# Cutting the later loads of a DMA-bound kernel into pieces of 16 rows and dealing them out between the stores

## The chip, the cores and the metric

One core of a Trainium2 chip runs the kernel. The metric is the device time of one execution in microseconds (us). All runs quoted here are of the fast state; profiles are one execution each, and a span in a profile is some 2 us shorter than the time of the same execution. "The queue" below is SyncE's instruction stream, which issues nearly all transfers (SPq in the profile); "the engines" without a name are the 16 DMA engines.

## The reference, cut to what matters

```python
_pairs = list(itertools.combinations(range(32), 2))        # 496 pairs (i, j)
v_i = inputs[:, I_IDX, :]                                   # inputs (1024, 32, 128)
v_j = inputs[:, J_IDX, :]
transformed = jnp.einsum('bpd,ped->bpe', v_i, W)            # W (496, 128, 128)
return transformed * v_j                                    # (1024, 496, 128), 260 MB
```

## The kernel before

Each pair is computed in two halves (steps u = 0 to 991) of 512 batch rows: TensorE multiplies, VectorE multiplies by the second field and writes an output tile, and after the second half SyncE stores that tile of 512 KB. All x stays on the chip once loaded; W comes in 62 chunks of eight pairs (512 KB) through three buffers. The parts that the change touches:

```python
opool = ctx.enter_context(tc.tile_pool(name="o", bufs=6))

def load_x(f, n=1, pieces=1, eng=None): ...       # t[:, :, ...] <- xt[:, f:f+n, ...], 1 MB for n=2
def load_w(c, splits=(0, WL)): ...                # w_raw[c] <- wt[c], 512 KB

# ... start-up loads ...
load_w(1)
load_x(NF - 6, 2)
# ... split_w, split_x, first(u) cut ...
def second(u):
    # ...
    nc.vector.tensor_tensor(ots[g][:, k, s], po.pop(u), x_sb[j][:, s], ALU.mult)
    # ...
    elif k == OG - 1 and h == 1:
        nc.sync.dma_start(out=out[g], in_=ots[g])

for u in range(2 * NQ + LAG):
    q = u // 2
    if u % (2 * WL) == 0 and (q // WL + WLEAD) * WL < NQ:
        load_w(q // WL + WLEAD)                   # every 16 steps
    if u < 2 * NQ:
        i, j = pairs[q]
        if u % 2 == 0 and j == i + 1 and i % 2 == 0 and 0 <= i - 2 - XLEAD:
            load_x(i - 2 - XLEAD, 2)
        first(u)
    if u >= LAG:
        second(u - LAG)
    # ...
```

## Time and profile before

| | before |
|---|---|
| median of the runs beside the changed kernel | 781.52 us (778.96 to 786.6) |
| profiled span | 775.5 us |
| bytes read, written | 49.3 MB, 260.0 MB |
| transfers issued by SyncE | 577 |
| DMA packets of the main queue, share of 16 engines | 83,088, 100.4% |

The DMA shares of the slices and stages say whether the engines are the bound; they are shown in the prediction. The timeline of the queue alone over 12 us (start, length, engine, line, operation, tile, count; a length over several instructions includes the gaps between them):

```profile
301.22 1.58 SPq L167 DMA_DIRECT2D out_dram<-ot  x2
302.90 1.09 SPq L83 DMA_DIRECT2D w<-in_wt_dram  x1
304.09 8.16 SPq L167 DMA_DIRECT2D out_dram<-ot  x6
```

The reader sees that the queue carries eight stores and a load in each period. A store's issue after a pause lasts 333 ns in the median of 296 cases, and 1.06 us in the median of 131 when it follows another store without one. From 30 us after the start to 30 us before the last issue, 709 us, issues and the short gaps between them fill 413 us; the other 296 us the queue waits for something to issue. 332 of 494 stores are issued within 0.1 us of the end of the VectorE instruction that completes their tile: mostly the queue waits for VectorE.

### The profile page before, as it was taken

What the parts mean: (1) busy time and instruction counts of PE and PEld (TensorE: products, weight loads), DVE (VectorE), ACT (ScalarE), POOL (GpSimd) and SP (SyncE); (2) the same over time, 40 slices, a digit from 0 to 9 for tenths busy, and PEclk for the clock granted to TensorE, in tenths of its full rate; (3) what the DMA queues carried; (4) which work ended last, traced back from release to release, by engine and by line L of the source; (5) the groups of instructions that cost most, each with busy time, mean ns of one, the idle gap of its engine ahead of it and who ended that gap; (6) DMA issues with size and microseconds to landing.
All of it is one profiled execution on the core that took longest, in us unless ns stands there. A gap on an engine that the chain in (4) does not pass through costs nothing.

```text
span 775.5 us, 11576 instructions
## 1 busy us (share of the span) xinstructions
PE 713.5 (92%) x2946; PEld 559.3 (72%) x2946; DVE 628.8 (81%) x992; ACT 616.6 (80%) x1136; POOL 550.7 (71%) x523
## 2 busy tenths in 40 slices
PE   7899889898997998998998999899999999999994
PEld 3477668786886876776876877688778778777773
DVE  4578769696887977887886897798988988889886
ACT  1279768797896997886986988699889889888883
POOL 0989997978686886875867595668676758585550
PEclk9999989999999999999999999899999999999998
DMA  9999999999999999999999999999999999999997
GB/s 354 418 374 408 416 382 391 403 409 403 403 407 396 408 405 417 393 392 410 409 399 408 393 405 397 394 395 404 411 406 406 409 405 404 414 405 398 410 415 318
DMA packets 83730, 310.10 MB, mean 400 GB/s; under 512 B 9296, under 2 KB 9424, under 8 KB 81872
## 3 DMA queue, kind: packets, MB, share of 16 engines
q1 hardware_dynamic: 83088, 308.32, 100.4%
q10 hardware_dynamic: 576, 1.05, 0.4%
q8 instruction: 23, 0.38, 0.2%
q14 instruction: 43, 0.35, 0.1%
HBM read 49.28 MB, written 260.05 MB: 399 GB/s over the span
## 4 chain that ended last, share of the span: by engine, by line
PE 44%; DMA 38%; DVE 12%; POOL 3%; issue 1%; DVEq 0%; ACT 0%; SPq 0%; POOLq 0%
DMA out_dram<-ot 35%; PE po L148 30%; PE po L157 14%; DVE ot L163 12%; DMA x<-in_xt_dram 2%; POOL xd L109 1%; POOL xl L107 1%; DMA w<-in_wt_dram 1%; POOL wl L93 0%; POOL xl L108 0%; POOL wd L95 0%; DVEq L163 0%; ACT xh L106 0%; POOL wd L94 0%; SPq L83 0%
## 5 line engine op out<-in xcount | busy, mean ns | idle before, releaser
L163 DVE TENSOR_TENSOR ot<-po,x 128x512 f32<-128x512 f32 x992 | 628.8, 686 | 139.5 <-DMA out_dram<-ot 90.7
L149 ACT ACTIVATE po<-po 128x512 f32<-128x512 f32 x962 | 538.9, 581 | 131.7 <-PE po L148 85.4
L148 PE MATMUL po<-xh,wh 128*128 128x512 f32 x962 | 387.0, 402 | 44.5 <-DVE ot L163 44.0
L148 PE MATMUL po<-xl,wl 128*128 128x512 f32 x962 | 380.7, 396 | 3.4 <-POOL wl L93 2.5
L157 PE MATMUL po<-xd,wd 128*128 128x512 f32 x962 | 379.9, 395 | 0.0
L93 POOL TENSOR_TENSOR wl<-w,wh 128x512 fp32r<-128x512 f32 x121 | 156.3, 1292 | 152.5 <-ACT wh L92 152.4
L148 PEld LDWEIGHTS po<-xh,wh 128*128 128x128 f32 x962 | 184.1, 191 | 105.5 <-DVE ot L163 66.3
L148 PEld LDWEIGHTS po<-xl,wl 128*128 128x128 f32 x962 | 184.6, 192 | 40.5 <-POOL wl L93 2.9
L157 PEld LDWEIGHTS po<-xd,wd 128*128 128x128 f32 x962 | 183.6, 191 | 39.8 <-ACT po L149 0.4
L95 POOL TENSOR_TENSOR wd<-wl,wd 128x512 fp32r<-128x512 f32 x121 | 156.7, 1295 | 10.1
L107 POOL TENSOR_TENSOR xl<-x,xh 128x512 fp32r<-128x512 f32 x52 | 67.3, 1293 | 22.8 <-ACT xh L106 22.8
L94 POOL TENSOR_SCALAR wd<-wh 128x512 fp32r<-128x512 f32 x121 | 75.2, 621 | 10.2
L92 ACT ACTIVATE wh<-w 128x512 fp32r<-128x512 f32 x121 | 75.7, 626 | 0.0
L109 POOL TENSOR_TENSOR xd<-xh,xl 128x512 fp32r<-128x512 f32 x52 | 67.0, 1289 | 4.3
L106 ACT ACTIVATE xh<-x 128x512 fp32r<-128x512 f32 x52 | 32.6, 630 | 14.1 <-DMA x<-in_xt_dram 14.1
L108 POOL TENSOR_SCALAR xl<-xl 128x512 fp32r<-128x512 f32 x52 | 32.3, 622 | 4.5
L145 PE MATMUL po<-x,w 128*128 128x512 f32 x60 | 28.7, 642 | 4.2 <-DMA x<-in_xt_dram 4.2
L145 PEld LDWEIGHTS po<-x,w 128*128 128x128 f32 x60 | 11.9, 204 | 20.1 <-issue 13.4
L106 ACT ACT_TABLE_LOAD x1 | 1.3, 1283 | 2.6 <-issue 2.6
L200 POOL MEMSET const-float32-0.0<- 128x1 f32 x1 | 0.1, 99 | 0.2 <-issue 0.2
L200 POOL MEMSET const-bfloat16-1.0<- 128x1 bf16 x1 | 0.1, 102 | 0.0
L200 POOL MEMSET const-uint8-127<- 128x1 uint8 x1 | 0.1, 102 | 0.0
(1 smaller groups left out, 0.1 us busy)
## 6 DMA issues: line engine op xcount, KB each, us to landing
out_dram<-ot SPq DMA_DIRECT2D x494, 512.0 KB, 7.3
w<-in_wt_dram SPq DMA_DIRECT2D x61, 512.0 KB, 7.1
x<-in_xt_dram SPq DMA_DIRECT2D x14, 1024.0 KB, 10.1
x<-in_xt_dram ACTq DMA_DIRECT2D x4, 256.0 KB, 5.7
x<-in_xt_dram SPq DMA_DIRECT2D x2, 512.0 KB, 6.9
out_dram<-ot SPq DMA_DIRECT2D x4, 256.0 KB, 6.1
w<-in_wt_dram SPq DMA_DIRECT2D x1, 448.0 KB, 4.7
w<-in_wt_dram SPq DMA_DIRECT2D x1, 64.0 KB, 3.1
```

The source lines that it names most:

```text
L92: nc.scalar.mul(h, raw, 1.0 - 2.0**-13)
L93: nc.gpsimd.tensor_tensor(l, raw, h.bitcast(F32), ALU.subtract)
L94: nc.gpsimd.tensor_scalar(d, h.bitcast(F32), EPS, 1.0, ALU.mult, ALU.mult)
L95: nc.gpsimd.tensor_tensor(d, l.bitcast(F32), d.bitcast(F32), ALU.subtract)
L106: nc.scalar.mul(h, x_sb[f][:, s], 1.0 - 2.0**-13)
L107: nc.gpsimd.tensor_tensor(l, x_sb[f][:, s], h.bitcast(F32), ALU.subtract)
L109: nc.gpsimd.tensor_tensor(d, h.bitcast(F32), l.bitcast(F32), ALU.subtract)
L145: nc.tensor.matmul(po[u], w_raw[q // WL][:, q % WL, :], x_sb[i][:, s], start=True, stop=True)
L148: nc.tensor.matmul(po[u], w_s[c][t][:, r], x_s[i][t][:, s], start=t == 0, stop=t == 1)
L149: nc.scalar.mul(po[u], po[u], 1.0 + EPS)
L157: nc.tensor.matmul(po[u], w_s[q // WC][2][:, r], x_s[i][2][:, s], start=False, stop=True, skip_group_check=True)
L163: nc.vector.tensor_tensor(ots[g][:, k, s], po.pop(u), x_sb[j][:, s], ALU.mult)
```

## The change

Its intent: a whole load of w leaves 128 data packets and 16 landings in the trace, so, counted evenly, eight packets in a row on each engine: 8 x 159 = 1,272 ns of its time between two stores. A piece of 16 rows leaves 16 data packets and again 16 landings, a single row on each engine, and one piece per step is issued between the stores. A pair takes two steps, so two pieces follow each store while a load is being dealt out.

```diff
     load_w(1)
     load_x(NF - 6, 2)
+    load_w(2)
+    load_x(NF - 8, 2)
+    pieces = []
+    LS = P // 16
+
+    def trickle(dst, src):
+        for k in range(LS):
+            pieces.append((dst[k::LS], src[k::LS]))
+
+    def load_x_slow(f, n):
+        t = xpool.tile([P, n, BT], F32, tag=f"x{f}", name=f"x_{f}")
+        for k in range(n):
+            x_sb[f + k] = t[:, k, :]
+        trickle(t, xt[:, f : f + n, :])
+
+    def load_w_slow(c):
+        w_raw[c] = rpool.tile([P, WL, P], F32, tag="w", name=f"w_{c}")
+        trickle(w_raw[c], wt[c])
@@ the loop over u
-        if u % (2 * WL) == 0 and (q // WL + WLEAD) * WL < NQ:
-            load_w(q // WL + WLEAD)
+        if u % (2 * WL) == 0 and q > 0 and (q // WL + WLEAD) * WL < NQ:
+            load_w_slow(q // WL + WLEAD)
...
-            if ... and i % 2 == 0 and 0 <= i - 2 - XLEAD:
-                load_x(i - 2 - XLEAD, 2)
+            if ... and i % 2 == 0 and i < NF - 2 and 0 <= i - 2 - XLEAD:
+                load_x_slow(i - 2 - XLEAD, 2)
             first(u)
         if u >= LAG:
             second(u - LAG)
+        if pieces:
+            dst, src = pieces.pop(0)
+            nc.sync.dma_start(out=dst, in_=src)
```

More of the change, by code (lines that the diff above doesn't have):

```diff
@@ L170 @@
         q = u // 2
-        if u % (2 * WL) == 0 and (q // WL + WLEAD) * WL < NQ:
-            load_w(q // WL + WLEAD)
+        if u % (2 * WL) == 0 and q > 0 and (q // WL + WLEAD) * WL < NQ:
+            load_w_slow(q // WL + WLEAD)
         if u < 2 * NQ:
             i, j = pairs[q]
-            if u % 2 == 0 and j == i + 1 and i % 2 == 0 and 0 <= i - 2 - XLEAD:
-                load_x(i - 2 - XLEAD, 2)
+            if u % 2 == 0 and j == i + 1 and i % 2 == 0 and i < NF - 2 and 0 <= i - 2 - XLEAD:
+                load_x_slow(i - 2 - XLEAD, 2)
             first(u)
```

## The prediction

> **What bounds the kernel now.** I read the page from the busy shares down, because the change moves only transfers: first who is busiest, then the DMA rows of the slices, then what the engines wait for, and last the single packets.
>
> ```profile
> PE 713.5 (92%) x2946; PEld 559.3 (72%) x2946; DVE 628.8 (81%) x992; ACT 616.6 (80%) x1136; POOL 550.7 (71%) x523
> ...
> DMA  9999999999999999999999999999999999999997
> ...
> DMA packets 83730, 310.10 MB, mean 400 GB/s; under 512 B 9296, under 2 KB 9424, under 8 KB 81872
> ...
> q1 hardware_dynamic: 83088, 308.32, 100.4%
> ...
> HBM read 49.28 MB, written 260.05 MB: 399 GB/s over the span
> ```
>
> No compute engine is full, but the DMA row is at 9 in every slice but the last, and the packets of the one queue that matters take 100.4% of 16 engines' span. The table by stage says the same with decimals (the columns are PE, PEld, DVE, ACT and POOL busy, then clock, DMA share and GB/s):
>
> ```profile
> 0.00:20.00 20.00, 15.85 (x31) 6.58 (x32) 8.53 (x14) 3.30 (x5) 1.48 (x5) 1.00 0.92 356
> 200.00:300.00 100.00, 93.63 (x401) 75.66 (x399) 82.68 (x131) 84.99 (x160) 77.82 (x74) 0.98 1.02 406
> 700.00:775.00 75.00, 63.93 (x274) 50.78 (x273) 62.09 (x98) 55.83 (x101) 31.98 (x30) 0.97 0.97 387
> ```
>
> From 60 to 700 us the share is 1.02: packets overlap a little and no engine has a gap. Only the start and the end fall short. The waits of VectorE and of the queue that issues transfers show how this reaches the engines:
>
> ```profile
> DVE ot L163 <- DMA out_dram<-ot: 90.7, 54, 5.0
> ...
> SPq L167 <- DVE ot L163: 444.2, 458, 5.9
> SPq L167 <- DMA x<-in_xt_dram: 13.9, 8, 2.8
> ...
> out_dram<-ot SPq DMA_DIRECT2D x494, 512.0 KB, 7.3
> w<-in_wt_dram SPq DMA_DIRECT2D x61, 512.0 KB, 7.1
> x<-in_xt_dram SPq DMA_DIRECT2D x14, 1024.0 KB, 10.1
> ```
>
> VectorE waits 90.7 us for an output buffer to be stored; there are six, a store takes 7.3 us to land, and TensorE stands behind VectorE. So the kernel is **bound by DMA engine time**, and I priced that from single packets. Of the 4 KB packets (71,296) the median is 159 ns; of the 8 KB packets (1,792, only x loads) 309 ns; a 4-byte semaphore packet (9,232) takes 9 ns. All packets at such normal durations are 752.3 us of 16 engines. They really took 778.4 us: **26.1 us is excess** in single slow packets, 18.6 us among the 4 KB and 7.3 us among the 8 KB ones, some of them 1 to 2 us long. About 86% of it lies in the stretches from 2.5 us before a load's first landing to its last. In 1 us bins that no load touches the engines move 416 GB/s, in bins full of them 384. That is the gap this change can hope to close: 310.1 MB at 416 GB/s is 745 us, with about 8 us of start and drain 753, or 22 us under the span.
>
> [...]9,296 landings are 16 for each of 581 transfers.
> - [...]This trace's slow packets reach 2.19 us.
> [...]
>
> **The change part by part.**
> 1. *Start: nothing.* The weights' chunk 2 and the x pair for NF-8 were issued at step 0, and still are, in the same order.
> 2. *Added transfers.* Chunks 3 to 61 of w become 59 x 8 = 472 pieces of 64 KB; the twelve later x pairs become 96 pieces of 128 KB. Instead of 71 transfers there are 568, so 497 more. Data packets keep number and size. 497 x 16 = 7,952 semaphore packets at 9 ns over 16 engines: **+4.5 us**, on the bound resource.
> 3. *Order on the engines.* Each engine used to meet a run of 8 load packets; now it meets one or two between 8-packet stores. I followed the packets of single engines by their ends and starts and sorted the runs by what landed at their end. In 533 runs of w packets the excess by place in the run was 46, 18, 11, 5, 10, 2, 4 and 0 ns, together 97; in 58 runs of x, 79, 49, 23, 29, 44, 73, 52 and 10, together 357. (Runs with long stalls are partly lost by this method.) The first load after stores pays most. If each dealt piece pays like a first or a second (32 ns for w, 64 for x), w costs 59 x (256 - 97) = 9.4 us more and x 12 x (508 - 357) = 1.8 us: **+11 us**. Against this, in the engines that are first at a run, while most others still store, the first packet's excess is 7 to 18 ns, not 46. A thinly spread read may therefore be cheap; then w costs 59 x (8 x 15 - 97) = 1.4 us more and nothing is gained or lost. With no excess at all, 86% of 26.1 = **-22 us**.
> 4. *Fewer bytes in flight.* Issue instructions walk through eight semaphores, and before each one the issuing engine waits for the transfer eight back. At present six stores and a load (3.0 MB on average, 5.6 transfers) fit within that. While pieces are dealt, two follow each store, so eight are 2.7 stores and 5.3 pieces: 1.4 + 0.35 = 1.75 MB for w, 4.3 us at 410 GB/s. A store[...] lands in about 2.6 us on a fast engine, which leaves 1.7 us for engines to differ; today first and last landing of a store lie 2.6 us apart (median). The fast engines will run dry at times in the roughly half of the steps that deal pieces. My estimate is 0.1 us for each of 59 chunks, **+6 us**; it could be nil or 20.
> 5. *Issue time.* A store takes 0.33 us to issue[...]. Two pieces and a store per 1.56 us are about 3 x 0.43 = 1.3 us with their waits: close, but it fits.
> 6. *Shorter delays of stores.* A 1 MB load holds up stores 2.5 us, and VectorE then waits up to 5 us. This shrinks, but TensorE steps at 0.68 us per half pair when it runs freely, 675 us for 992, so it has slack and waits that only mirror the DMA bound give nothing back.
>
> Sum of the middle case: 4.5 + 6 for reads (between 1.4 and 11) + 6 - 12 of burst excess (a guess: about half of what could be won[...]) = about +4 us on 779.9.
>
> **The rivals.**
> - *The burst excess goes away*: the 384 against 416 GB/s speaks for it, and the cheap first packets of leading engines. That the loads at the start, which meet no stores, have almost no excess for w speaks against: mixing with stores does the harm, and dealing mixes more. It would give 780 - 22 + 4.5, about 762.
> - *Eight transfers in flight become the bound*, or weights arrive late: the last piece of a chunk is issued 7 steps after the first, and ScalarE asks for it some 11 steps later, being several ahead of the stores. Waits of ScalarE for w, of which there are none now, would take the place of some of VectorE's. 800 to 815.
> - *Transfers are hidden anyway*: engine time is the same, only its order differs; 780 to 785.
> [...]
>
> **The range.** The middle is 784 us, as gains and costs nearly cancel. 763 is the burst excess gone; 808 is the in-flight limit with dearer reads. Within 2% is 764.3 to 795.5. I give faster 0.2, same 0.5, slower 0.3, as more of the single terms point up than down.
>
> **What would show it.** Step 2: the number of 4-byte packets must rise by 7,952, to 17,184 in the main queue. Step 3: the sum of packet times, 100.4% of the span now, against packets' normal times; 8 KB packets above 309 ns. Step 4: a DMA share under 1.02 in the middle stages and waits of the issuing queue for DMAs much above today's 20 us. Step 5: issue instructions of a piece over 0.5 us. The lateness rival: waits of ScalarE for w. The prediction fails if the reads' excess vanishes (share still 1.02, GB/s at 415) or if the share falls to 0.95.

The sum is 4.5 + 6 + 6 - 12 = +4.5 us on 779.9, hence 784. The -12 stays the author's guess from the 22 us that could be won.

What step 4 builds on is in the trace of before. Its transfers, SyncE's and the four that ScalarE issues at the start, take eight semaphores in turn: for 567 of 573 the one eight back has the same. None of the 573 was issued before the last one on its semaphore had landed. From 60 to 700 us 5.7 transfers are in flight on average. Every store had at least three other transfers in flight; the ten quickest first landings came 2.46 to 2.57 us after the issue. Step 5: its 0.33 us is the median issue of a store after a pause, its 0.43 us that of a load of x at the start (0.42 to 0.43). And for the first rival's loads at the start: the 384 packets of 4 KB that begin in the first 11 us, before any store, average 161 ns, 2 above the median; in the 533 runs of w it was 97 / 8 = 12.

## The result, and the profile after

The changed kernel takes **872.64 us** (872.22 to 874.9, 4 runs) where the kernel before took 781.52. The ratio is 1.116, with a 95% interval of 1.110 to 1.123. A ratio here is the mean time of one kernel's fast runs over that of the other's of the same rounds, so it isn't quite the ratio of the medians. The result is correct.

The page of the changed kernel, the lines that answer to those of before:

```profile
PE 765.0 (88%) x2946; PEld 541.9 (62%) x2946; DVE 636.6 (73%) x992; ACT 614.7 (70%) x1136; POOL 549.6 (63%) x523
...
DMA packets 91690, 310.19 MB, mean 355 GB/s; under 512 B 17248, under 2 KB 17376, under 8 KB 89824
...
q1 hardware_dynamic: 91040, 308.35, 94.6%
...
DMA 47%; DVE 19%; PE 17%; SPq 10%; issue 3%; POOL 2%; DVEq 1%; ACT 0%; ACTq 0%; POOLq 0%
...
out_dram<-ot SPq DMA_DIRECT2D x494, 512.0 KB, 4.0
w<-in_wt_dram SPq DMA_DIRECT2D x473, 64.0 KB, 3.1
x<-in_xt_dram SPq DMA_DIRECT2D x96, 128.0 KB, 4.4
```

Nothing is busier than before: every compute engine lost share, and so did the DMA engines, 94.6% against 100.4%. A store lands 4.0 us after its issue where it took 7.3. That is the first hint that transfers no longer stand in line at the engines but come too slowly: from 60 to 700 us 4.7 are in flight on average, before 5.7. SPq also has 10% of the chain that ended last. The table by stage has the share of the engines at 0.95, with fewer GB/s:

```profile
300.00:400.00 100.00, 88.33 (x346) 63.21 (x345) 72.94 (x115) 74.30 (x139) 66.45 (x64) 0.98 0.95 352
```

And the queue's own waits and its timeline:

```profile
SPq L188 <- DVE ot L184: 156.9, 272, 2.7
SPq L203 <- POOL wd L94: 16.1, 29, 1.0
...
SPq L188 <- DMA x<-in_xt_dram: 3.8, 2, 2.1
```

The first of these lines misleads. The view counts a wait up to the last semaphore update that falls before the end of the issue instruction, also where that instruction had long begun. Of all waits in this view 167 us lie inside issue instructions that were already running, and only 19 us before their start (before: 169 and 304 us). The tiles themselves say it plainly: in the changed kernel 4 of 494 stores are issued within 0.1 us of their tile's completion, and the median tile stands ready for 4.7 us before its store begins. The queue hardly waits for VectorE any more.

```profile
304.30 0.54 SPq L188 DMA_DIRECT2D out_dram<-ot  x1
304.89 1.54 SPq L203 DMA_DIRECT2D w<-in_wt_dram  x2
306.53 0.58 SPq L188 DMA_DIRECT2D out_dram<-ot  x1
307.15 1.26 SPq L203 DMA_DIRECT2D w<-in_wt_dram  x2
308.51 0.54 SPq L188 DMA_DIRECT2D out_dram<-ot  x1
309.09 1.32 SPq L203 DMA_DIRECT2D w<-in_wt_dram  x2
```

Each row begins where the one before it ends, but for some 50 ns. From a store over two pieces to the next store it is 2.07 us in the median of 231 such rounds of w. (About one in five, nearly always the first of a chunk, behind a run of stores, takes 3.9 us.) In that round the queue hands each engine 8 + 2 packets of 159 ns, **1.59 us of work for 2.07 us of issuing**. Over the stretch that is chosen as above the queue is now occupied for 804 of 809 us. It was 413 of 709: 497 more transfers cost it 391 us (0.79 us each), of which 291 us fit into the time in which it used to wait, and 100 us came out as time.

On the engines' side: the profiled span has grown by 97.6 us, from 775.5 to 873.1, while the packets of the main queue took 825.6 us of 16 engines where they took 778.4. So about 50 us of the growth are times in which engines have no packet, 43 us are packets that took longer than their normal time, and 4.5 us are the added semaphore packets. Engines do run dry, then, but nearly half of the loss shows up as slower packets.

So the theory to test, **A: the changed kernel is bound by the time that the one queue needs to issue transfers, whatever they carry.** Its rivals: **B**, reads that are mixed with stores cost the DMA engines more; **C**, the choice of rows does, as a piece takes rows 8 apart; and **D**, the weights arrive late. ScalarE waits for w, which it never did before:

```profile
ACT wh L92 <- DMA w<-in_wt_dram: 75.5, 42, 7.6
```

D can be judged from the tiles already: if late weights set the pace, the tiles would be late, and the queue would stand waiting for them. They stand ready for it, 4.7 us in the median.

### The profile page after: what moved, and what is told of

Read it like the earlier page. It is cut to its first block, busy times and chain, and to the rows that moved or that the text cites. A ratio compares the mean times of both kernels' runs of the same rounds, so it can differ in the third digit from the quotient of the medians.

```text
span 873.1 us, 12427 instructions
## 1 busy us (share of the span) xinstructions
PE 765.0 (88%) x2946; PEld 541.9 (62%) x2946; DVE 636.6 (73%) x992; ACT 614.7 (70%) x1136; POOL 549.6 (63%) x523
## 3 DMA queue, kind: packets, MB, share of 16 engines
q1 hardware_dynamic: 91040, 308.35, 94.6%
## 4 chain that ended last, share of the span: by engine, by line
DMA 47%; DVE 19%; PE 17%; SPq 10%; issue 3%; POOL 2%; DVEq 1%; ACT 0%; ACTq 0%; POOLq 0%
DMA out_dram<-ot 45%; DVE ot L184 19%; PE po L169 12%; SPq L203 8%; PE po L178 5%; SPq L188 2%; DMA w<-in_wt_dram 1%; DMA x<-in_xt_dram 1%; POOL wl L93 1%; DVEq L184 1%; POOL xd L109 0%; POOL wd L94 0%; ACT po L170 0%; POOL wd L95 0%; POOL xl L107 0%
## 5 line engine op out<-in xcount | busy, mean ns | idle before, releaser
L184 DVE TENSOR_TENSOR ot<-po,x 128x512 f32<-128x512 f32 x992 | 636.6, 687 | 229.3 <-DMA out_dram<-ot 139.9
L170 ACT ACTIVATE po<-po 128x512 f32<-128x512 f32 x962 | 530.7, 578 | 124.0 <-PE po L169 86.4
L169 PE MATMUL po<-xh,wh 128*128 128x512 f32 x962 | 405.8, 422 | 70.0 <-DVE ot L184 67.1
L178 PE MATMUL po<-xd,wd 128*128 128x512 f32 x962 | 384.6, 400 | 21.4 <-ACT po L170 21.3
L92 ACT ACTIVATE wh<-w 128x512 fp32r<-128x512 f32 x121 | 76.0, 629 | 107.2 <-DMA w<-in_wt_dram 75.5
```

What stands on the lines that cost most here:

```text
L92: nc.scalar.mul(h, raw, 1.0 - 2.0**-13)
L169: nc.tensor.matmul(po[u], w_s[c][t][:, r], x_s[i][t][:, s], start=t == 0, stop=t == 1)
L170: nc.scalar.mul(po[u], po[u], 1.0 + EPS)
L178: nc.tensor.matmul(po[u], w_s[q // WC][2][:, r], x_s[i][2][:, s], start=False, stop=True, skip_group_check=True)
```

## The experiments

Eleven kernels ran, each beside the kernel before on the same chip, in three rounds. All results were correct. Differences to the kernel before are of medians.

| run | transfers issued by SyncE | time, us | before, us | queue's waiting time, us | DMA share |
|---|---|---|---|---|---|
| before (profile) | 577 | | | 296 | 1.004 |
| changed kernel | 1074 | 872.6 | 781.5 | 5 | 0.946 |
| e1_tiny | 1074 | 913.8 | 780.1 | 43 | 0.925 |
| e5_split | 826 | 923.2 | 780.1 | 343 | 0.906 |
| e6_at_once | 1074 | 983.4 | 779.9 | 5 | 0.854 |
| e4_neighbours | 1074 | 826.0 | 780.1 | 20 | 0.986 |
| e2_rows32 | 790 | 795.6 | 780.1 | 21 | 0.999 |
| e3_rows64 | 648 | 783.7 | 779.9 | 321 | 1.002 |
| e8_columns | 648 | 783.9 | 779.9 | 381 | 1.005 |
| e7_neigh64 | 648 | 794.0 | 779.9 | 400 | 1.009 |
| e9_after_pairs | 827 | 825.2 | 780.5 | 54 | 0.967 |
| e10_before_pairs | 330 | 800.7 | 780.5 | 613 | 0.976 |
| e11_tiny_neigh | 1074 | 892.5 | 780.5 | 68 | 0.947 |

(The waiting time is the sum of the queue's gaps over 0.13 us, away from both ends. The DMA share is the main queue's packet time over the span of 16 engines.)

### e1_tiny: the issues without the pieces

The loads stay whole. At the steps where the changed kernel deals pieces, SyncE issues 497 loads of 2 KB that nobody reads.

```diff
+    tt = tpool.tile([P, 12, 32], F32, tag="tiny", name="tiny")
+    def tiny_pieces():
+        for _ in range(LS - 1):
+            k = n_tiny[0] % 12; n_tiny[0] += 1
+            pieces.append((tt[0:P:LS, k, :], xt[0:P:LS, 0, 0:32]))
-        trickle(w_raw[c], wt[c])
+        nc.sync.dma_start(out=w_raw[c], in_=wt[c])
+        tiny_pieces()
```

> The kernel before with its whole loads, plus 497 tiny loads (16 rows of 128 B, nobody reads them) issued by the same engine at the steps where the changed kernel deals its pieces. Theory A (the queue that issues transfers is the bound: each further transfer costs it 0.5 to 0.9 us, whatever it carries): 850 to 880 us, the issuing engine without a gap, about 2.0 us from a store over two tiny loads to the next store. Theory B (the engines read dearer when reads are mixed with stores): the loads are not mixed any more than before, so 780 to 790. Theory C[...]: 780 to 790, as the tiny rows move next to nothing.

Measured: 913.8 us, even slower than the changed kernel. B and C expected no loss, as hardly a byte moves otherwise than before. A had the direction and the round right (2.11 us from a store over two tiny loads to the next store, 2.0 expected), but the time was 34 us over its range, and the queue was not without a gap: it waited 43 us. An estimate made afterwards gives about the difference to the changed kernel: 71 of the changed kernel's 568 pieces are here whole loads, whose issue took 1.15 us in the median instead of some 0.6 us, and 71 x 0.55 = 39 us. The view of the issues shows the whole loads and the 497 tiny ones:

```profile
w<-in_wt_dram SPq DMA_DIRECT2D x61, 512.0 KB, 6.1
x<-in_xt_dram SPq DMA_DIRECT2D x14, 1024.0 KB, 8.1
tiny<-in_xt_dram SPq DMA_DIRECT2D x497, 2.0 KB, 3.7
```

A tiny load's issue instruction lasts 492 ns when it follows a store, the very number of the changed kernel's pieces: a transfer that carries 2 KB costs as much to issue as one that carries 64. It lasts 492 ns after a pause too (44 cases), so the pause makes no difference to it.

### e6_at_once: pieces without dealing

```diff
-        if pieces:
+        while pieces:
             dst, src = pieces.pop(0)
```

> The same 568 pieces of 16 rows, but all pieces of one load are issued at once, where the whole load stood, instead of one per step. Theory A: the queue has as many transfers to issue as in the changed kernel, so nearly the same time, 850 to 880. Theory B (dealing the reads between the stores is what costs): most of the loss goes, 785 to 810.

Measured: 983.4 us, the slowest of all. B is refuted, since here the reads aren't mixed with the stores any more than before. D falls too: no wait of ScalarE for w is left, as the pieces are issued up to seven steps earlier, and yet the time is longer. A expected 850 to 880 and was wrong by 100 us. Why shows in the queue's timeline:

```profile
310.48 6.55 SPq L203 DMA_DIRECT2D w<-in_wt_dram  x8
317.13 8.11 SPq L188 DMA_DIRECT2D out_dram<-ot  x8
325.33 6.35 SPq L203 DMA_DIRECT2D w<-in_wt_dram  x8
331.77 7.99 SPq L188 DMA_DIRECT2D out_dram<-ot  x8
```

A period is the sum of eight pieces and eight stores, 6.4 and 8.0 us. The last six pieces of each eight last 587 ns and bring 0.16 us of work per engine, and the engines run dry (the DMA share is 0.85); the stores afterwards last about 1.15 us each, behind one another (a store brings 8 x 159 ns = 1.27 us of work). In the changed kernel a store behind a piece lasts 0.53 us; why dealing makes the issues shorter, no run shows. What is shown is that **the dealing was the good half of the change (983 to 873 us), and cutting into 568 transfers the bad one**.

### e2_rows32 and e3_rows64: fewer, larger pieces

```diff
-    LS = P // 16
+    LS = P // 32        # e3_rows64: P // 64
```

> Pieces of 32 rows, two rows per engine: 284 pieces in place of 568, the rest as changed. A: the issuing engine has some 12.5 us for 8 stores and 4 pieces, needs about 8, so it is no longer the bound and the time falls to 778 to 795. B: the excess goes with the number of pieces, so half of the 91 us stay: 820 to 835. C: [...]about 870.

> Pieces of 64 rows (every second one), four rows per engine: 142 pieces. Theory A (issue time of the one queue is the bound of the changed kernel, DMA engine time comes next): one store and one or two pieces no longer fill the queue, so the time is the DMA bound, 775 to 788. If dealing itself does harm on the DMA engines, the 15 us that 284 pieces of 32 rows still cost halve to 8: 785 to 790. If dealing helps the DMA engines, as the 416 against 384 GB/s seemed to say, under 772.

Measured: 795.6 us for 284 pieces (just over A's upper end) and 783.7 us for 142 (within A's range). So the loss over the kernel before goes 3.8, 15.5 and 91.1 us for 142, 284 and 568 pieces: not with the number, as B had it, and not unchanged, as C had it, but with a knee. One reading needs care: the queue of the 32-row pieces waits hardly more than that of the changed kernel, 21 us, and yet nothing much is lost. There the engines are full (0.999), and the issues are long (a store's is 0.87 us in the median); what lengthens them, no run shows. So a queue that hardly waits isn't by itself the bound here: with 21 us of waits and engines at 0.999 the loss is 15.5 us, with 5 us of waits and engines at 0.946 it is 91.1.

The 142 pieces also answer the question of the intent. Their excess of slow packets, as the prediction defined it, is 29.9 us where the kernel before has 26.1, and bins full of loads move 382 GB/s, before 384. **Dealing the loads does not make the reads cheaper.**

### e8_columns and e7_neigh64: which rows

```diff
-    LS = P // 16
+    LS = 2
 # e7_neigh64
-            pieces.append((dst[k::LS], src[k::LS]))
+            pieces.append((dst[64 * k : 64 * k + 64], src[64 * k : 64 * k + 64]))
 # e8_columns
-            pieces.append((dst[k::LS], src[k::LS]))
+            h = dst.shape[1] // 2
+            pieces.append((dst[:, k * h : (k + 1) * h, :], src[:, k * h : (k + 1) * h, :]))
```

> Two pieces per load that keep all 128 rows and take half of the columns, dealt. A: no more issue time than 142 pieces of 64 rows[...]: 772 to 785, the best of the dealt kernels.[...]

> Two pieces of 64 neighbouring rows per load, dealt. Same count as the pieces of every second row. Pieces of 16 neighbours were 47 us faster than 16 rows 8 apart; if that comes from issue time alone, it is hidden here and the time equals that of every second row within 1%, 775 to 788. If it comes from the engines' way into SBUF[...], this one is slower by 1% or more.

Measured: 783.9 us for half of the columns of all 128 rows, the same as every second row (783.7), so not the best of the dealt kernels. (This edit also halves the packets: 2 KB for w, 4 KB for x.) 64 neighbouring rows cost 794.0 us, 10 us or 1.3% more, though the queue has more time to spare (400 against 321 us). The engines' packet time is 799.9 against 782.8 us, and the 8 KB packets of x average 492 ns against 396. So which rows a piece takes does matter to the engines, as C says, but as some 10 us at 142 pieces, and in a kernel whose queue has 400 us to spare. The reason isn't shown; that it is the way into SBUF was the author's assumption, and the rows' places in HBM changed too.

### e4_neighbours and e11_tiny_neigh: 16 neighbouring rows

```diff
 # e4_neighbours
-            pieces.append((dst[k::LS], src[k::LS]))
+            pieces.append((dst[16 * k : 16 * k + 16], src[16 * k : 16 * k + 16]))
 # e11_tiny_neigh, from e1_tiny
-            pieces.append((tt[0:P:LS, k, :], xt[0:P:LS, 0, 0:32]))
+            pieces.append((tt[0:16, k, :], xt[0:16, 0, 0:32]))
```

> Pieces of 16 neighbouring rows in place of rows 8 apart, the same count and order. A: the same number of transfers to issue, 868 to 878. B: about the same, perhaps a little less, as 16 neighbouring rows of w are one stretch of 64 KB. C: [...]a clear loss: 890 and more.

> The first run's tiny loads (914 us), but of 16 neighbouring rows in place of rows 8 apart. If the pieces of neighbouring rows (826 against 872 us) gain by shorter issue alone, the same gain shows here, where next to no data moves: 860 to 880. If they gain by the way the data takes, nothing changes: 905 to 920.

Measured: 826.0 us for the pieces, 46.6 us under the changed kernel with the same number of transfers. C expected a loss, A no difference, B at most a little less; none had it. The issue of such a piece behind a store lasts 435 ns, not 492, and that of a store behind a piece 372 ns, not 525; the round from store to store is 1.86 us, not 2.07. So the time to issue depends here on which rows are taken, not on the count alone, and 275 rounds (231 of w, 44 of x) x 0.21 = 58 us is somewhat more than the gain. With tiny loads, where next to no data moves, neighbouring rows gain too, but 21 us (892.5 against 913.8), short of the 34 to 54 expected. So part of the gain is shown to be issue time; whether the rest has to do with the data, or with the queue's longer waits in that run (68 us), stays open.

### e9_after_pairs and e10_before_pairs: fewer stores

This takes issue time away and leaves every piece and its rows as they are: outputs are stored two pairs at a time.

```diff
-OG = 1
+OG = 2
-    opool = ctx.enter_context(tc.tile_pool(name="o", bufs=6))
+    opool = ctx.enter_context(tc.tile_pool(name="o", bufs=3))
```

> The changed kernel with all its 568 pieces, but with outputs stored two pairs at a time (1 MB in rows of 8 KB, three buffers in place of six): 249 stores to issue in place of 498, the same bytes, the same pieces[...]. Theory A: between two stores the queue has four pieces to issue, about 3.0 us, while the engines have 3.2 us of work, so most of the loss goes: within 25 us of the kernel before with the same stores (next run). If each piece costs its time on the DMA engines and not in the issuing queue, the loss of some 90 us against that run stays.

> The kernel before with outputs stored two pairs at a time, the control for the run above. DMA engine time is the same less 249 x 16 semaphore packets; three large buffers release less finely than six: 775 to 805.

Measured: 825.2 us with the pieces and 800.7 without. The pair of kernels differs by **24.6 us where it differed by 91.1**, with the same 568 pieces in both. That is just within A's limit of 25; a fixed cost of each piece on the engines would have stayed. And 90 of 247 stores are again issued within 0.1 us of their tile's completion (246 of 247 in the control). But A's arithmetic for the round was off: a store with four pieces of w takes 4.62 us in the median, not about 3.0, for some 3.1 us of the engines' work. The queue makes it up in rounds without pieces, 0.98 us for 2.5 us of work. The edit also doubles the bytes that stand behind each store's issue, so by itself it doesn't part issue time from a limit on the bytes in flight. For comparison with the stages above:

```profile
300.00:400.00 100.00, 88.31 (x362) 67.01 (x361) 74.68 (x122) 77.85 (x141) 66.94 (x63) 0.98 0.98 373
```

The larger stores themselves cost 20 us (three coarse buffers in place of six), so this is no improvement over the kernel before.

### e5_split: half of the tiny loads from another engine

```diff
-            nc.sync.dma_start(out=dst, in_=src)
+            (nc.scalar if n_issued[0] % 2 else nc.sync).dma_start(out=dst, in_=src)
+            n_issued[0] += 1
```

> As the first run, but every second tiny load is issued by ScalarE's queue, the others by SyncE's. A in the form that the limit is each issuing engine's own: 780 to 810, well under the first run. A in the form [...]: as the first run, 850 to 880. B and C: as the first run and as the kernel before, 780 to 790.

Measured: 923.2 us (three fast runs; 923.6 with the slow one), no better than the first run, and outside both forms' ranges. This was to tell a limit of each issuing engine (780 to 810) from one that both share (850 to 880), and it doesn't: SyncE's queue has 343 us to spare here, so its issues aren't the bound. What is, its waits show:

```profile
SPq L165 <- DMA tiny<-in_xt_dram: 116.8, 42, 5.6
SPq L202 <- DMA out_dram<-ot: 72.1, 111, 2.2
SPq L202 <- DMA tiny<-in_xt_dram: 58.6, 39, 3.9
```

Over all lines SyncE waits 227 us for tiny loads. In the traces before and after, both engines take their transfers' semaphores in turn from the same eight, and no transfer is issued before the last one on its semaphore has landed (573 and 1,070 cases). If that holds here, each engine waits for transfers that the other may not have issued yet; that these are SyncE's waits is the author's reading, not shown. Moving issues to another engine brought a new wait. Whether the limit is each engine's own stays open, so "the queue's issue time" here means what its issue instructions last, whatever sets it.

## Why the prediction was wrong

Measured was a ratio of 1.116, with 784 us predicted and 808 as the upper end. By its own steps:

1. **Step 5, issue time, failed, and it is the miss.** From the 0.33 us of a 128-row store after a pause it took 0.43 us with waits for every issue, a piece of 16 rows too: "Two pieces and a store per 1.56 us are about 3 x 0.43 = 1.3 us with their waits: close, but it fits". The round took 2.07 us: 525 ns for the store behind a piece, 492 for the first piece, 840 for the second (587 in e6_at_once, from the third piece of a row of them on), and gaps. A transfer of one row per engine isn't cheaper to issue than one of eight rows here; it is dearer (492 against 333 ns, both after a pause). The prediction called the step close and then gave it no term in the sum, no rival and no part of the range. It did name the sign, "issue instructions of a piece over 0.5 us", and that came. The slower packets (43 of the 97.6 us) are not derived from it; item 4 has what is known of them. The pieces of w that were nearly free here (142 pieces in all, 3.8 us) have 256 KB, but no run tells their size from their number.
2. Step 1, the start, held: the first stage moves 354 GB/s where it moved 356.
3. Step 2 held to the packet: 17,184 packets of 4 bytes, and the normal packet time rose from 752.3 to 756.8 us, by the 4.5 said.
4. Step 3 had two terms. The dearer first reads were put at 1 to 11 us: at 142 pieces the excess is 3.8 us above that of before. The 12 us to be won from bursts weren't there: 29.9 and 28.3 us of excess with 142 pieces, 26.1 with whole loads. In the changed kernel the excess is 69 us and in e6_at_once 81, but also in e1_tiny 80.6, which deals no loads; so it goes along with many small transfers and engines that run dry, and isn't a mark of dealing. What slows these packets stays open.
5. Step 4, eight transfers in flight, was not the bound. In the view of waits the queue's waits for DMAs fell from 22 to 12 us, and in nine of ten issues the transfer eight back had landed at least 1 us earlier. The lower DMA share that it foretold came, 0.95, but from the queue. Nor does the share tell what the bound is: e5_split has 0.906 and the changed kernel 0.946, and only the queue's gaps, 343 and 5 us, told them apart.
6. The rival of late weights was seen (75.5 us of ScalarE's waiting) but as a consequence: in e6_at_once it is gone, and the kernel is 111 us slower; in the changed kernel the finished tiles wait for the queue. The rival about rows 8 apart was not tested for them, as the pieces of 16 rows are bound by issue time. 64 neighbouring rows cost about 10 us in e7_neigh64.

No run here beats the kernel before. It is bound by the engines' packet time, 778.4 us, and none of the ways to cut its loads lowered that (782.8 us with 142 pieces, 825.6 with 568).

## What to carry to other kernels

Price a change in the number of transfers in the queue that issues them: sum the lengths of its issue instructions over a round, compare with the engine work that the round hands out, and do not assume that a small transfer is quick to issue: here one of 2 KB took 492 ns, a store of 512 KB after a pause 333. Here each of 497 more transfers cost the queue 0.79 us; 291 us of that fitted into the queue's waiting, and 100 us came out as time. To see whether a queue is the bound, look at whether finished work stands ready before its issue begins. In this kernel two pieces per load were nearly free to deal (3.8 us), four cost 15.5 us, and eight 91.1 us.
